# Last stages of an AdaLN and mixture-of-experts kernel: three sets of token blocks instead of two halves, strips of 256 tokens in the last two

## The chip, the cores and the metric

One core of a Trainium2 chip runs the whole program. The metric is the device time of one execution in microseconds (us). Data are float32 throughout.

## The reference

The input is 32 sequences of 128 tokens with 128 features, 4096 tokens. Two layers follow each other, and each adds its result to the input. The change touches the second layer (L1) only, so the first is given in one line.

```python
x = x + ffn0(cond0(x))                      # layer 0: gated experts with 512 hidden features
# layer 1, conditional part, for every token
shared = sum(silu(x @ w1[e].T) * (x @ w3[e].T) @ w2[e].T for e in range(2)) / 2    # hidden 256
routed = sum(gelu(x @ r1[e].T) @ r2[e].T * gate[:, e] for e in range(8))           # hidden 128
y = (shared + routed) / 4
# layer 1, low-rank part (rank 32, hidden 512)
p = y @ U1
h = gelu_tanh(p @ V1 + b1)
q = h @ U2
x = x + q @ V2 + b2
```

The gates of the routed experts come from a router that picks two of eight for each token; the kernel computes every expert for every token and multiplies by the gate, which is zero for the others.

## The kernel before

Tokens are kept transposed: features on the 128 partitions, tokens along the free dimension, in eight blocks of 512 tokens (`TB`), four blocks to a half (`SB = 4`, two halves). Layer 0 ends at about 825 us. What follows is a list of units that `pipelined` (L200) works through: it calls the first step (`up`) of unit i + 1, then the second step (`down`) of unit i, then whatever `after` (L926) hangs on unit i. The order of the list (L916 to L924) is thus the order of the program; within it a scheduler may still move an instruction of an engine ahead of another that it does not depend on.

There are three kinds of units. A shared unit (`sh_up`, L846) takes one 128-wide piece of the hidden features of the shared experts, for the four blocks of a half: for each block two products `g1` and `u1`, silu of the first on ScalarE, and the product of both on VectorE into the tile `hs`. A routed unit (`r_up`, L869) takes one routed expert: for each block the gate row is broadcast to all partitions by GpSimd (`spread`, L634, tile `rg`), one product `ur`, exact gelu on ScalarE (`ar`), and the multiply by the gate on VectorE (`hr`). Both kinds end in `into` (L841). The down projection and the rank-32 projection U1 have been folded beforehand into one matrix of 128 x 32 for each unit (`fold`), so `into` adds 32 rows for each block into one PSUM tile `p_ps`: block j of the half stands on partitions 32j to 32j + 31, all units of the half accumulate there. These matmuls use 32 columns of the array each, four side by side. The wide products are also cut into four matmuls of 32 columns (`by_columns`, L231).

A low-rank unit (`low_up`, L889, and `low_down`, L899) takes 128 of the 512 hidden features of the low-rank part: for each of the four strips one matmul `ul` from its 32 partitions of `pT` (the copy of `p_ps` in SBUF, `low_in`, L884), so 32 rows of the array and all columns, then gelu (tanh form, another table of ScalarE than silu and than exact gelu) with a bias into `hl`, and back by `into` to 32 rows in the PSUM tile `q_ps`. `low_out` (L904) copies `q_ps` to `qT`, does the last product `o_ps`, adds bias and residual on VectorE (`fin`, L912), and sends each block to HBM, in turn from the SP and the ScalarE queue.

The order of the units is: shared units of both halves; the eight routed units of half 0; two of half 1; three low-rank units of half 0; the other six routed units of half 1; the last low-rank unit of half 0; the four low-rank units of half 1; and `low_out(1)`.

Buffers in rotation: products in PSUM (`mm`) six, PSUM sums (`p_ps`, `q_ps`) two, `h` tiles (`hs`, `hr`, `hl`) three, outputs of ScalarE (`s1`, `ar`) four, broadcast gates four, `fin` four.

Of the kernel before, what the change touches and what calls it, by code (L numbers as in the profile page):

```python
# [44 lines left out]
SB = 4  # L45
NS = NB // SB
NT = B * S // P
H = 512
NC = H // P
E0, EF, E1 = 4, 8, 8  # L50
# [43 lines left out]
AT32, NCOLS32 = columns(COLS32)  # L94
# [5 lines left out]
def adaln_ffn(  # L100
# [3 lines left out]
    nc = tc.nc  # L104
    V = nc.vector
# [4 lines left out]
    work = ctx.enter_context(tc.tile_pool(name="work", bufs=2))  # L110
# [14 lines left out]
    par32 = const([P, NCOLS32], "par32")  # L125
# [12 lines left out]
    ident = const([P, P], "ident")  # L138
# [92 lines left out]
    def by_columns(ps, w, x, n):  # L231


        for at in range(0, P, n):
            own = slice(at, at + n)
            nc.tensor.matmul(ps[own, :], lhsT=w[:, own], rhs=x, start=True, stop=True)  # L236

# [3 lines left out]
    fold = const([P, 4 + E1, 32], "fold")  # L241
# [312 lines left out]
    def gates_to_dram(kind, sb):  # L554

        gates, name = held.pop((kind, sb)), f"{kind}g{sb}"
        ps = mm_tile(f"{name}_ps")
        nc.tensor.transpose(ps[:, :P], gates.rearrange("p e b -> p (e b)"), ident)
        t = work.tile([P, P], F32, tag="gsb", name=f"{name}_sb", bufs=1)
        V.tensor_copy(t, ps[:, :P])  # L560
        d = dram.tile([P, P], F32, tag=name, name=name)
        nc.sync.dma_start(out=d, in_=t)
        in_dram[kind, sb] = d.rearrange("(g k b) t -> k g (b t)", g=2, k=4)
# [44 lines left out]
    held, in_dram, fgates = {}, {}, {}  # L608
# [20 lines left out]
    units = [("s", b) for b in range(FIRST)] + [("p", q) for q in range(NUNIT)]  # L629
# [4 lines left out]
    def spread(row, name):  # L634

        bc = work.tile([P, TB], F32, tag="bc", name=name, bufs=4)
        nc.gpsimd.partition_broadcast(bc, row)  # L637
        return bc

    def glu(ps_gate, ps_up, h, name):  # L640
        s = work.tile([P, TB], F32, tag="sg", name=name, bufs=4)
        nc.scalar.activation(s, ps_gate, AF.Silu)  # L642
        V.tensor_tensor(h, s, ps_up, ALU.mult)  # L643
# [178 lines left out]
    sws_t = [wpool.tile([P, 2, 2, P], F32, tag=f"sw{i + 1}", name=f"sws{i}") for i in range(2)]  # L822
    rw1_t = wpool.tile([P, E1, P], F32, tag="w3", name="rw1_t")
# [3 lines left out]
    x1T = xT  # L827
# [8 lines left out]

    low_p = [y_tile(f"p_ps{sb}") for sb in range(NS)]

    def into(y, w, h, first, last):  # L841

        for j in range(SB):
            nc.tensor.matmul(y[32 * j : 32 * (j + 1), :], lhsT=w, rhs=h[:, j, :], start=first, stop=last)  # L844

    def sh_up(sb, k):  # L846
        e, c = divmod(k, 2)
        h = work.tile([P, SB, TB], F32, tag="h", name=f"hs_{sb}_{k}", bufs=3)
        for j in range(SB):
            x = x1T[SB * sb + j]  # L850
            g, u = mm_tile(f"g1_{sb}_{k}_{j}"), mm_tile(f"u1_{sb}_{k}_{j}")
            by_columns(g, sws_t[0][:, e, c, :], x, 32)
            by_columns(u, sws_t[1][:, e, c, :], x, 32)
            glu(g, u, h[:, j, :], f"s1_{sb}_{k}_{j}")
        return h

    def sh_down(sb, k, h):
        into(low_p[sb], fold[:, k, :], h, k == 0, False)


    grows = [
        wpool.tile([P, 2, SB * TB], F32, tag=tag, name=f"grows{sb}") for sb, tag in enumerate(("wg", "wu"))
    ]

    def gate_rows(sb):
        for k in range(4):
            nc.sync.dma_start(out=grows[sb][32 * k : 32 * k + 1, :, :], in_=in_dram["r", sb][k : k + 1, :, :])

    def r_up(sb, e):  # L869
        h = work.tile([P, SB, TB], F32, tag="h", name=f"hr_{sb}_{e}", bufs=3)  # L870
        g, k = divmod(e, 4)
        for j in range(SB):
            gate = spread(grows[sb][32 * k : 32 * k + 1, g, j * TB : (j + 1) * TB], f"rg_{sb}_{e}_{j}")
            ps = mm_tile(f"ur_{sb}_{e}_{j}")
            by_columns(ps, rw1_t[:, e, :], x1T[SB * sb + j], 32)
            a = work.tile([P, TB], F32, tag="sg", name=f"ar_{sb}_{e}_{j}", bufs=4)
            nc.scalar.activation(a, ps, AF.Gelu)  # L877
            V.tensor_tensor(h[:, j, :], a, gate, ALU.mult)  # L878
        return h

    def r_down(sb, e, h):
        into(low_p[sb], fold[:, 2 * 2 + e, :], h, False, e == E1 - 1)

    def low_in(sb):  # L884
        t = work.tile([P, TB], F32, tag="pT", name=f"pT{sb}", bufs=1)
        V.tensor_copy(t, low_p[sb])
        held["p", sb] = t

    def low_up(sb, c):  # L889
        h = work.tile([P, SB, TB], F32, tag="h", name=f"hl_{sb}_{c}", bufs=3)  # L890
        at = AT32["v1"].start + c * P
        for j in range(SB):
            ps = mm_tile(f"ul_{sb}_{c}_{j}")
            own = slice(32 * j, 32 * (j + 1))
            nc.tensor.matmul(ps, lhsT=par32[own, at : at + P], rhs=held["p", sb][own, :], start=True, stop=True)  # L895
            nc.scalar.activation(h[:, j, :], ps, AF.Gelu_apprx_tanh, bias=col("b1", c))
        return h

    def low_down(sb, c, h):  # L899
        if c == 0:  # L900
            held["q", sb] = y_tile(f"q_ps{sb}")
        into(held["q", sb], col("u2", c * 32, 32), h, c == 0, c == NC - 1)

    def low_out(sb):  # L904
        q = work.tile([P, TB], F32, tag="lgT", name=f"qT{sb}", bufs=1)
        V.tensor_copy(q, held["q", sb])
        for j in range(SB):
            ps = mm_tile(f"o_ps{sb}_{j}")
            own = slice(32 * j, 32 * (j + 1))
            nc.tensor.matmul(ps, lhsT=par32[own, AT32["v2"]], rhs=q[own, :], start=True, stop=True)  # L910
            t = work.tile([P, TB], F32, tag="fin", name=f"fin{sb}_{j}", bufs=4)
            V.scalar_tensor_tensor(t, ps, col("b2"), x1T[SB * sb + j], ALU.add, ALU.add)  # L912
            queue = nc.sync if j % 2 == 0 else nc.scalar
            queue.dma_start(out=out[SB * sb + j], in_=t)

    STAGES = {"s": (sh_up, sh_down), "r": (r_up, r_down), "l": (low_up, low_down)}  # L916
    units = [("s", sb, k) for sb in range(NS) for k in range(4)]
    units += [("r", 0, e) for e in range(E1)]
    units += [("r", 1, 0), ("r", 1, 1)]
    units += [("l", 0, c) for c in range(NC - 1)]  # L920
    units += [("r", 1, e) for e in range(2, E1)]

    units += [("l", 0, NC - 1)]
    units += [("l", 1, c) for c in range(NC)]  # L924

    def after(kind, sb, i):  # L926
        if (kind, sb, i) == ("s", 0, 0):
            gate_rows(0)

            l1_scores(1)  # L930
        if (kind, sb, i) == ("s", 0, 2):
            route(1)
        if (kind, sb, i) == ("s", 1, 0):
            gates_to_dram("r", 1)
            gate_rows(1)
        if kind == "r" and i == E1 - 1:
            low_in(sb)
        if (kind, sb, i) == ("l", 0, NC - 1):
            low_out(0)

    def unit_up(kind, *at):
        return STAGES[kind][0](*at)
# [1 line left out]
    def unit_down(kind, *at):  # L944
        STAGES[kind][1](*at)

    pipelined(units, unit_up, unit_down, after)
    low_out(1)


# [77 lines left out]
```

## Time and profile before

| what | value |
|---|---|
| median of 3 runs | 978.38 us (978.09 to 978.49) |
| profiled execution, its own time | 979.06 us |
| its span, first to last instruction | 977.3 us |
| mean granted clock of TensorE | 0.998 |
| routed experts: `ur`, records of TensorE | 512, of 592 ns |
| `p_ps` and `q_ps` records | 192 and 64, of 592 ns |
| `ul` records | 64, of 588 ns |
| gelu of the low-rank part, 128x512 | 32 times, 689 ns |
| exact gelu of the routed part, 128x512 | 64 times, 597 ns |
| multiply by the gate on VectorE | 64 times, 674 to 1152 ns |
| broadcast on GpSimd | 64 times, 797 to 1340 ns |
| final add on VectorE (`fin`) | 8 times, 743 ns |
| table loads of ScalarE after 820 us | 6, of 1283 ns |

A matmul of float32 appears as two records in the trace. Records of the same engine overlap: those of four neighbouring column or row groups of 32 run at the same time, so the duration of a record says how long it is in the array, and the distance between the starts of groups says what it costs. A weight load (PEld) of the next matmul runs beside the matmul before it where the trace shows the two overlapping.

### The profile page before, as it was taken

What the parts mean: (1) busy time and instruction counts of PE and PEld (TensorE: products, weight loads), DVE (VectorE), ACT (ScalarE), POOL (GpSimd) and SP (SyncE); (2) the same over time, 40 slices, a digit from 0 to 9 for tenths busy, and PEclk for the clock granted to TensorE, in tenths of its full rate; (3) what the DMA queues carried; (4) which work ended last, traced back from release to release, by engine and by line L of the source; (5) the groups of instructions that cost most, each with busy time, mean ns of one, the idle gap of its engine ahead of it and who ended that gap; (6) DMA issues with size and microseconds to landing.
All of it is one profiled execution on the core that took longest, in us unless ns stands there. A gap on an engine that the chain in (4) does not pass through costs nothing.

```text
span 977.3 us, 15574 instructions
## 1 busy us (share of the span) xinstructions
PE 962.9 (99%) x5998; PEld 450.8 (46%) x5998; DVE 630.5 (65%) x1130; ACT 345.0 (35%) x615; POOL 142.2 (15%) x151
## 2 busy tenths in 40 slices
PE   7999999999999999999999999999999999999997
PEld 3588974444444444444444444444444443323342
DVE  3444565666866776686676786567667656648593
ACT  5455544223322322232232332222223224335764
POOL 1000001100101011110101011010100001009680
PEclk9999999999999999999999999999999999999999
DMA  9745650000000000000000000000000000000002
GB/s 319 234 132 153 211 182 26 2 1 4 2 1 1 1 1 1 1 2 1 1 2 1 1 2 3 1 1 1 1 1 2 1 3 2 1 7 1 2 1 87
DMA packets 19043, 34.05 MB, mean 35 GB/s; under 512 B 1729, under 2 KB 9921, under 8 KB 18945
## 3 DMA queue, kind: packets, MB, share of 16 engines
q1 hardware_dynamic: 18096, 31.43, 10.3%
q10 hardware_dynamic: 864, 1.52, 0.4%
q8 instruction: 52, 0.85, 0.4%
q14 instruction: 31, 0.25, 0.1%
HBM read 30.59 MB, written 2.36 MB: 34 GB/s over the span
## 4 chain that ended last, share of the span: by engine, by line
PE 84%; DVE 2%; DVEq 0%; issue 0%
PE u L236 25%; PE g L236 25%; PE ya L729 10%; PE yb L729 8%; PE ur L236 6%; PE p_ps L844 2%; PE ul L895 1%; PE us L260 1%; PE ys L271 1%; PE q_ps L844 1%; PE y L513 0%; PE u L497 0%; DVE hf L704 0%; PE fold_ps L247 0%; DVE t L705 0%; DVE t L706 0%
## 5 line engine op out<-in xcount | busy, mean ns | idle before, releaser
L642 ACT ACTIVATE sf<-g 128x512 f32<-128x512 f32 x256 | 152.7, 597 | 438.1 <-PE g L236 432.0
L643 DVE TENSOR_TENSOR hf<-sf,u 128x512 f32<-128x512 f32 x256 | 174.9, 686 | 185.7 <-PE u L236 184.7
L236 PE MATMUL g<-c0all,wg_t 128*64 128x512 f32 x1024 | 270.3, 593 | 0.0
L236 PE MATMUL u<-cg,wu_t 128*64 128x512 f32 x1024 | 270.1, 592 | 0.0
L637 POOL PARTITION_BROADCAST fg<-fgT x64 | 71.9, 1135 | 662.4 <-DVE cg L685 499.1
L236 PEld LDWEIGHTS u<-cg,wu_t 128*64 128x64 f32 x1024 | 75.7, 137 | 145.2 <-issue 124.4
L236 PEld LDWEIGHTS g<-c0all,wg_t 128*64 128x64 f32 x1024 | 75.7, 137 | 120.2 <-issue 108.2
L729 PE MATMUL ya<-t,wd_t 128*64 128x256 f32 x512 | 121.6, 379 | 0.1
L637 POOL PARTITION_BROADCAST rg<-grows x64 | 67.8, 1187 | 145.4 <-DVE hr L878 76.8
L878 DVE TENSOR_TENSOR hr<-ar,rg 128x512 f32<-128x512 f32 x64 | 60.7, 996 | 15.8 <-ACT ar L877 15.8
L729 PEld LDWEIGHTS ya<-t,wd_t 128*64 128x64 f32 x512 | 69.9, 137 | 0.7 <-DVE t L706 0.6
L500 ACT ACTIVATE h<-u,w 128x256 f32<-128x256 f32 (+3 forms) x136 | 50.3, 429 | 54.3 <-PE u L497 54.3
L729 PE MATMUL yb<-hf,a_sum 128*64 128x256 f32 x512 | 69.1, 379 | 0.0
L729 PE MATMUL ya<-t,a_sum 128*64 128x256 f32 x256 | 65.9, 379 | 0.0
L729 PE MATMUL ya<-hf,wd_t 128*64 128x256 f32 x256 | 65.8, 379 | 0.0
L704 DVE TENSOR_TENSOR hf<-hf 128x512 f32<-128x512 f32 x64 | 62.7, 979 | 2.1
L236 PE MATMUL ur<-xall,rw_t 128*32 128x512 f32 x512 | 58.4, 592 | 0.0
L729 PEld LDWEIGHTS ya<-hf,wd_t 128*64 128x64 f32 x256 | 34.9, 137 | 42.8 <-issue 31.9
L513 PE MATMUL y<-h,w 128*128 128x256 f32 (+3 forms) x272 | 53.1, 338 | 1.0 <-DVE t L516 1.0
L497 PE MATMUL u<-x,w 128*128 128x256 f32 (+3 forms) x272 | 53.0, 338 | 1.1 <-DVEq L478 1.1
L497 PEld LDWEIGHTS u<-x,w 128*128 128x128 f32 x272 | 45.3, 190 | 5.7 <-ACT h L500 1.3
L877 ACT ACTIVATE ar<-ur 128x512 f32<-128x512 f32 x64 | 37.9, 598 | 27.6 <-PE ur L236 27.3
(215 smaller groups left out, 961.4 us busy)
## 6 DMA issues: line engine op xcount, KB each, us to landing
w<-in_experts SPq DMA_DIRECT2D x36, 514.5 KB
xall<-in_x SPq DMA_DIRECT2D x8, 256.0 KB
wg_t<-in_w_gate SPq DMA_DIRECT2D x8, 256.0 KB
wu_t<-in_w_up SPq DMA_DIRECT2D x8, 256.0 KB
wd_t<-in_w_down SPq DMA_DIRECT2D x8, 256.0 KB
out<-fin SPq DMA_DIRECT2D x4, 256.0 KB
out<-fin ACTq DMA_DIRECT2D x4, 256.0 KB
downs<-in_r_w SPq DMA_DIRECT2D x2, 256.0 KB
```

What stands on the lines that cost most here:

```text
L236: nc.tensor.matmul(ps[own, :], lhsT=w[:, own], rhs=x, start=True, stop=True)
L497: nc.tensor.matmul(ps[c][:, :m, :n], lhsT=w1, rhs=x[:, :m, :n], start=True, stop=True)
L500: nc.scalar.activation(h[:, c, :m, :n], ps[c][:, :m, :n], AF.Gelu_apprx_tanh, bias=bias)
L513: nc.tensor.matmul(y[:, :m, :n], lhsT=w2, rhs=h[:, c, :m, :n], start=(c == 0), stop=(c == NC - 1))
L637: nc.gpsimd.partition_broadcast(bc, row)
L642: nc.scalar.activation(s, ps_gate, AF.Silu)
L643: V.tensor_tensor(h, s, ps_up, ALU.mult)
L704: V.tensor_tensor(b12, b12, b11, ALU.subtract)
L729: nc.tensor.matmul(y[half, n], lhsT=w[:, c, :], rhs=h[:, c, :], start=False, stop=(e == EF - 1 and last))
L844: nc.tensor.matmul(y[32 * j : 32 * (j + 1), :], lhsT=w, rhs=h[:, j, :], start=first, stop=last)
L877: nc.scalar.activation(a, ps, AF.Gelu)
L878: V.tensor_tensor(h[:, j, :], a, gate, ALU.mult)
```

## The change

The eight blocks are now three sets (`group` in the code): set 0, blocks 0 to 3 as before; set 1, blocks 4 and 5; set 2, blocks 6 and 7. In the last two sets the four strips of 32 partitions in `p_ps`, `q_ps`, `pT` and `qT` hold half a block each, 256 tokens, so `p_ps` and `q_ps` matmuls, `ul` and the low-rank gelu are 256 wide there. A shared unit of these sets takes two blocks; a routed unit takes two experts with two blocks each, so it still has four products. The low-rank units of a set stand among the shared units of the next one: two shared, two low-rank, two shared, then two low-rank (after set 0) or one (after set 1, whose last one comes behind all routed units). The output of set 0 is made after the first routed unit of set 1, all on the SP queue; the output of set 1 among the low-rank units of set 2. The gates of the second half go to HBM and back after the second routed unit of set 0. For the last set, the residual of two of the four half blocks is put into PSUM ahead of time by a matmul with the identity (`out_begin`); ScalarE finishes these two with the bias, VectorE the other two, and each half block is sent by itself (`out_end`). All matmuls of 32 columns or 32 rows in these stages are kept in the order in which the program states them.

```diff
@@ by_columns
-            nc.tensor.matmul(ps[own, :], lhsT=w[:, own], rhs=x, start=True, stop=True)
+            mm = nc.tensor.matmul(ps[own, :], lhsT=w[:, own], rhs=x, start=True, stop=True)
+            if n < 64:
+                tc.keep_in_program_order(mm)
...
+    GROUPS = ((0, 4, TB), (4, 2, TB // 2), (6, 2, TB // 2))
+    low_p, low_q_ps = {}, {}
+    def in_order(mm):
+        tc.keep_in_program_order(mm)
-    def into(y, w, h, first, last):
-        for j in range(SB):
-            nc.tensor.matmul(y[32 * j : 32 * (j + 1), :], lhsT=w, rhs=h[:, j, :], start=first, stop=last)
+    def into(y, w, strips, first, last):
+        for j, h in enumerate(strips):
+            in_order(nc.tensor.matmul(y[32 * j : 32 * (j + 1)], lhsT=w, rhs=h, start=first, stop=last))
+    def strips_of(h, group):
+        n = GROUPS[group][2]
+        return [h[:, b, at : at + n] for b in range(h.shape[1]) for at in range(0, TB, n)]
...
+    def experts_of(group, i):
+        return (i,) if group == 0 else (2 * i, 2 * i + 1)
+    def r_up(group, i):
+        h = work.tile([P, SB, TB], F32, tag="h", name=f"hr_{group}_{i}", bufs=3)
+        pieces = [(e, b) for e in experts_of(group, i) for b in blocks(group)]
...
+    def r_down(group, i, h):
+        n = GROUPS[group][1]
+        for at, e in enumerate(experts_of(group, i)):
+            own = h[:, at * n : (at + 1) * n, :]
+            into(low_p[group], fold[:, 2 * 2 + e, :], strips_of(own, group), False, e == E1 - 1)
...
+    def by_rows(ps, w, t, j, first=True):
+        own = slice(32 * j, 32 * (j + 1))
+        in_order(nc.tensor.matmul(ps, lhsT=par32[own, w], rhs=t[own, :], start=first, stop=True))
+    def low_up(group, c):
+        h = work.tile([P, SB, TB], F32, tag="h", name=f"hl_{group}_{c}", bufs=3)
+        n = GROUPS[group][2]
+        v1 = AT32["v1"].start + c * P
+        for j in range(SB):
+            ps = mm_tile(f"ul_{group}_{c}_{j}")[:, :n]
+            by_rows(ps, slice(v1, v1 + P), held["p", group], j)
+            tc.keep_in_program_order(
+                nc.scalar.activation(h[:, j, :n], ps, AF.Gelu_apprx_tanh, bias=col("b1", c))
+            )
+        return h
...
+    def low_out(group, strips):
+        for j in strips:
+            b, at = strip(group, j)
+            ps = mm_tile(f"o_ps{group}_{j}")[:, : at.stop - at.start]
+            by_rows(ps, AT32["v2"], held["qT", group], j)
+            if at.start == 0:
+                t = work.tile([P, TB], F32, tag="fin", name=f"fin{b}", bufs=4)
+            V.scalar_tensor_tensor(t[:, at], ps, col("b2"), x1T[b][:, at], ALU.add, ALU.add)
+            if at.stop == TB:
+                nc.sync.dma_start(out=out[b], in_=t)
+    def out_begin():
+        for j in (1, 3):
+            b, at = strip(2, j)
+            held["o", j] = mm_tile(f"o_x{b}")[:, : TB // 2]
+            in_order(nc.tensor.matmul(held["o", j], lhsT=ident, rhs=x1T[b][:, at], start=True, stop=False))
+    def out_end():
         for j in range(SB):
+            b, at = strip(2, j)
+            ps = held["o", j] if j % 2 else mm_tile(f"o_ps{b}")[:, : TB // 2]
+            by_rows(ps, AT32["v2"], held["qT", 2], j, first=j % 2 == 0)
+            t = work.tile([P, TB], F32, tag="fin", name=f"fin_{j}", bufs=4)
+            if j % 2 == 0:
+                V.scalar_tensor_tensor(t[:, at], ps, col("b2"), x1T[b][:, at], ALU.add, ALU.add)
+                nc.sync.dma_start(out=out[b][:, at], in_=t[:, at])
+            else:
+                nc.scalar.activation(t[:, at], ps, AF.Identity, bias=col("b2"))
+                nc.scalar.dma_start(out=out[b][:, at], in_=t[:, at])
...
-    units = [("s", sb, k) for sb in range(NS) for k in range(4)]
-    units += [("r", 0, e) for e in range(E1)]
-    units += [("r", 1, 0), ("r", 1, 1)]
-    units += [("l", 0, c) for c in range(NC - 1)]
-    units += [("r", 1, e) for e in range(2, E1)]
-    units += [("l", 0, NC - 1)]
-    units += [("l", 1, c) for c in range(NC)]
+    units = [("s", 0, k) for k in range(4)] + [("r", 0, e) for e in range(E1)]
+    for group in (1, 2):
+        before_r = [("s", group, k) for k in range(4)]
+        low = [("l", group - 1, c) for c in range(NC)]
+        units += before_r[:2] + low[:2] + before_r[2:] + (low[2:] if group == 1 else low[2:3])
+        units += [("r", group, i) for i in range(E1 // 2)]
+    units += low[3:] + [("l", 2, c) for c in range(NC)]
...
-        if (kind, sb, i) == ("s", 1, 0):
+        if (kind, sb, i) == ("r", 0, 1):
             gates_to_dram("r", 1)
             gate_rows(1)
-        if kind == "r" and i == E1 - 1:
+        if kind == "r" and experts_of(sb, i)[-1] == E1 - 1:
             low_in(sb)
-        if (kind, sb, i) == ("l", 0, NC - 1):
-            low_out(0)
+        if kind == "l" and i == NC - 1:
+            low_q(sb)
+        if (kind, sb, i) == ("r", 1, 0):
+            low_out(0, range(SB))
+        if (kind, sb, i) == ("l", 2, 0):
+            low_out(1, (0, 1))
+        if (kind, sb, i) == ("l", 2, 1):
+            low_out(1, (2, 3))
+        if (kind, sb, i) == ("l", 2, 2):
+            out_begin()
...
-    low_out(1)
+    out_end()
```

More of the change, by code (lines that the diff above doesn't have):

```diff
@@ L834, in adaln_ffn, with blocks, sh_up, sh_down @@
         rest.pop(0)()
-    low_p = [y_tile(f"p_ps{sb}") for sb in range(NS)]
-    def into(y, w, h, first, last):
-        for j in range(SB):
-            nc.tensor.matmul(y[32 * j : 32 * (j + 1), :], lhsT=w, rhs=h[:, j, :], start=first, stop=last)
-    def sh_up(sb, k):
-        e, c = divmod(k, 2)
[L848 to L854, printed above, removed]
-        return h
-    def sh_down(sb, k, h):
-        into(low_p[sb], fold[:, k, :], h, k == 0, False)
+    GROUPS = ((0, 4, TB), (4, 2, TB // 2), (6, 2, TB // 2))
[8 more added lines that the diff above has]
+        return [h[:, b, at : at + n] for b in range(h.shape[1]) for at in range(0, TB, n)]
+    def blocks(group):
+        first, n, _ = GROUPS[group]
+        return range(first, first + n)
+    def sh_up(group, k):
+        e, c = divmod(k, 2)
+        h = work.tile([P, SB, TB], F32, tag="h", name=f"hs_{group}_{k}", bufs=3)
+        for at, b in enumerate(blocks(group)):
+            g, u = mm_tile(f"g1_{b}_{k}"), mm_tile(f"u1_{b}_{k}")
+            by_columns(g, sws_t[0][:, e, c, :], x1T[b], 32)
+            by_columns(u, sws_t[1][:, e, c, :], x1T[b], 32)
+            glu(g, u, h[:, at, :], f"s1_{b}_{k}")
+        return h
+    def sh_down(group, k, h):
+        _, n, size = GROUPS[group]
+        if k == 0:
+            low_p[group] = y_tile(f"p_ps{group}")[:, :size]
+        into(low_p[group], fold[:, k, :], strips_of(h[:, :n, :], group), k == 0, False)
     grows = [
@@ L867, in gate_rows @@
             nc.sync.dma_start(out=grows[sb][32 * k : 32 * k + 1, :, :], in_=in_dram["r", sb][k : k + 1, :, :])
-    def r_up(sb, e):
-        h = work.tile([P, SB, TB], F32, tag="h", name=f"hr_{sb}_{e}", bufs=3)
-        g, k = divmod(e, 4)
-        for j in range(SB):
[L873 to L878, printed above, removed]
-        return h
@@ L881, in r_down @@
[L881 to L891, printed above, removed]
-        for j in range(SB):
[L893 to L914, printed above, removed]
@@ new lines, in r_up @@
+    def r_up(group, i):
+        h = work.tile([P, SB, TB], F32, tag="h", name=f"hr_{group}_{i}", bufs=3)
+        pieces = [(e, b) for e in experts_of(group, i) for b in blocks(group)]
+        for at, (e, b) in enumerate(pieces):
+            g, k = divmod(e, 4)
+            sb, j = divmod(b, SB)
+            gate = spread(grows[sb][32 * k : 32 * k + 1, g, j * TB : (j + 1) * TB], f"rg_{b}_{e}")
+            ps = mm_tile(f"ur_{b}_{e}")
+            by_columns(ps, rw1_t[:, e, :], x1T[b], 32)
+            a = work.tile([P, TB], F32, tag="sg", name=f"ar_{b}_{e}", bufs=4)
+            nc.scalar.activation(a, ps, AF.Gelu)
+            V.tensor_tensor(h[:, at, :], a, gate, ALU.mult)
+        return h
@@ new lines, in r_down, with low_in @@
+    def r_down(group, i, h):
[3 more added lines that the diff above has]
+            into(low_p[group], fold[:, 2 * 2 + e, :], strips_of(own, group), False, e == E1 - 1)
+    def low_in(group):
+        t = work.tile([P, TB], F32, tag="pT", name=f"pT{group}", bufs=1)[:, : GROUPS[group][2]]
+        V.tensor_copy(t, low_p[group])
+        held["p", group] = t
+    def by_rows(ps, w, t, j, first=True):
+        own = slice(32 * j, 32 * (j + 1))
+        in_order(nc.tensor.matmul(ps, lhsT=par32[own, w], rhs=t[own, :], start=first, stop=True))
@@ new lines, in low_up, with low_down @@
+    def low_up(group, c):
+        h = work.tile([P, SB, TB], F32, tag="h", name=f"hl_{group}_{c}", bufs=3)
+        n = GROUPS[group][2]
+        v1 = AT32["v1"].start + c * P
+        for j in range(SB):
+            ps = mm_tile(f"ul_{group}_{c}_{j}")[:, :n]
[3 more added lines that the diff above has]
+            )
+        return h
+    def low_down(group, c, h):
+        n = GROUPS[group][2]
+        if "q" not in low_q_ps:
+            low_q_ps["q"] = y_tile("q_ps")
+        strips = [h[:, j, :n] for j in range(SB)]
+        into(low_q_ps["q"][:, :n], col("u2", c * 32, 32), strips, c == 0, c == NC - 1)
@@ new lines, in low_q, with strip @@
+    def low_q(group):
+        n = GROUPS[group][2]
+        q = work.tile([P, TB], F32, tag="lgT", name=f"qT{group}", bufs=1)[:, :n]
+        V.tensor_copy(q, low_q_ps["q"][:, :n])
+        held["qT", group] = q
+    def strip(group, j):
+        first, n, size = GROUPS[group]
+        b, half = divmod(j, SB // n)
+        return first + b, slice(half * size, (half + 1) * size)
+    def low_out(group, strips):
[8 more added lines that the diff above has]
+                nc.sync.dma_start(out=out[b], in_=t)
```

## The prediction

> **What bounds the kernel now.** I read the page first, then a table by stage of the last 100 us, then the chain of waits, and last the timelines of ScalarE, VectorE and GpSimd in the same place.
>
> ```profile
> span 977.3 us, 15574 instructions
> ...
> PE 962.9 (99%) x5998; PEld 450.8 (46%) x5998; DVE 630.5 (65%) x1130; ACT 345.0 (35%) x615; POOL 142.2 (15%) x151
> ...
> PE 84%; DVE 2%; DVEq 0%; issue 0%
> ```
>
> TensorE sets the time over the whole program; the first 825 us are not touched, so only the last 152 us count. The table by stage (busy PE, PEld, DVE, ACT, POOL, then granted clock, DMA share, GB/s):
>
> ```profile
> 875.00:918.00 43.00, 43.00 (x408) 12.84 (x400) 36.09 (x41) 24.39 (x42) 39.51 (x38) 1.00 0.01 2
> 918.00:925.10 7.10, 7.10 (x55) 2.40 (x56) 1.39 (x2) 7.07 (x12) 2.71 (x3) 1.00 0.00 0
> 925.10:950.00 24.90, 24.90 (x236) 12.56 (x232) 21.68 (x22) 15.92 (x27) 20.90 (x20) 1.00 0.01 2
> 950.00:977.30 27.30, 20.33 (x112) 5.68 (x104) 9.71 (x14) 13.81 (x22) 0.57 (x1) 0.92 0.21 77
> ```
>
> The last 27.3 us are a tail: TensorE counts as busy but does 112 records, where 24.9 us of routed experts hold 236. ScalarE fills the second row. The chain (start, us) shows what the pieces cost:
>
> ```profile
> 917.16 0.86 PE p_ps L844 x8
> 918.02 1.07 PE ul L895 x8
> 919.09 1.40 PE p_ps L844 x8
> ...
> 946.55 3.43 PE ur L236 x32
> 949.99 0.86 PE p_ps L844 x8
> ...
> 966.12 3.45 PE q_ps L844 x15
> ...
> 970.34 1.18 PE o_ps L910 x8
> ```
>
> A group of four strips of 512 tokens (8 records) takes 0.858 (3.43/4); I call it Q. The low-rank matmuls use 32 rows, the others 32 columns: going in costs about 0.2 (1.07 against 0.86), coming out 0.13 to 0.2. The `q_ps` of 3.45 is one Q stretched by waiting for ScalarE.
>
> ```profile
> 917.84 1.28 ACT L896 ACT_TABLE_LOAD   x1
> 919.14 7.17 ACT L896 ACTIVATE hl<-ul,par 128x512 f32<-128x512 f32 x12
> 926.33 1.28 ACT L877 ACT_TABLE_LOAD   x1
> ```
>
> Twelve activations in 7.17, 0.57 apart in the steady part: four need 2.3, more than the 1.7 of their two Q. And in the routed stage:
>
> ```profile
> 928.32 9.84 DVE L878 TENSOR_TENSOR hr<-ar,rg 128x512 f32<-128x512 f32 x10 [8.94 <-ACT ar L877]
> 929.10 9.72 POOL L637 PARTITION_BROADCAST rg<-grows  x9 [8.40 <-DVE hr L878]
> ```
>
> After two free starts (0.60 apart) a multiply by the gate and a broadcast move in step, 1.067 us a pair: 4.27 for the four of a unit, against 4.29 on TensorE (five Q). VectorE has no room there to make up a delay.
>
> **The change, part by part.** I count Q up to the end of the last `ur`, which is 949.99 before, then the tail.
>
> *Work moved.* From 825.03 to 949.99 the old order does 48 Q of shared `g`/`u`, 8 of their `p_ps`, 1 of `l_ps`, 64 of `ur`, 14 of their `p_ps`, 3 of `ul`, 3 of `q_ps`: 141 Q, 121.0 us; the other 3.9 are 1.4 at `l_b`, 0.3 at `rg_ps`, 1.9 in the low-rank block (7.08 for six Q), and rounding. The new order does before its last `ur` the same 48, 8, 1, 64, 14, and 5.5 `ul`, 5.5 `q_ps`, 1 `o_ps` (a 256-wide group is half a Q): 147 Q, or **+5.15**.
>
> That a 256-wide group runs at full rate is not shown for 32 columns. The nearest row is L729 (128x256, 64 columns): pairs of records 0.216 apart, weight loads of 137 ns hidden. I take 0.216 for four records of 32 columns, whose loads are shorter (110). Ends: nothing, or the load exposed, 0.11 on each of 46 such record groups (16 of shared units, 24 of routed, 6 of `q_ps`), 5.1 us. A gain is excluded, the array does the same columns.
>
> *Overheads in front of the last `ur`.* `l_b`, `rg_ps`: 1.9, 0.2 more than before, because the lone `p_ps` strip that ran while VectorE copied `l1T` is now pinned behind it. Set 0's low-rank units, first pair, time from the end of the last `u`: `p_ps` to 0.43, `ul` with its switch to 1.5; the tanh table is there at 1.1 (silu ends 0.2 before `u` does in this trace, load 1.28, small gap); four activations from 1.7 end at 4.1; only then can the last strip of `q_ps` start, end 4.95. Ideal is four Q, 3.43, so 1.5 lost. Second pair: here the listing of waits puts a PE wait on the table load itself, so it starts after `ul` (1.8), activations from 3.1, `q_ps` ends 6.3: 2.9 lost. `o_ps` of set 0 between routed units: two switches, 0.4. Set 1's first pair, half as wide (0.36 an activation, below): 1.0; its third unit: 0.4. Sum 8.1 against 3.9, **+4.2**. The other table loads (14 in these stages instead of 6) lie beside at least 3.4 us of `g`/`u` or `ur`, with six PSUM buffers in rotation; without that cover they would be 1.28 each.
>
> Here a rule speaks against the change. The Trainium skill (ScalarE: Activation LUTs, What ACT_TABLE_LOAD costs) counts about 1.38 us of drain on top of 1283 ns for each switch. The trace has the load at 926.33, right behind an activation that ends at 926.32, and the next activation at 927.62: 1.29 from end to start. By the row, the two loads in front of `q_ps` cost what stands above; by the rule those and the two that delay the last routed stage would add 4 x 1.4, 5.5 us. I take the row.
>
> *The four output adds of set 0* (`fin`, 0.66 apart) and the `qT` copy now sit on VectorE among set 1's multiplies, 3.3 us where it has no spare time. `p_ps` of a unit comes 4.29 after that unit's last `ur`; its multiply normally ends about 1.9 after it, and `o_ps` gives another 1.3. Behind the adds are queued eight multiplies; by my count they end 0.1 to 0.8 before their strips of `p_ps` can start. So nothing; from 0 to +0.7 if the adds compete with broadcasts (multiplies with a PSUM operand, L643, keep 686 ns beside broadcasts, so I take 0). Their DMAs go to SP, with nothing behind that is awaited. Set 1's gates (transpose `rg_ps`, a copy, five DMAs on SP) move from the second shared unit to the second routed one of set 0, where they are issued near 856 and first read near 905: hidden by ten units; without that cover each us of their way would be a us of set 1's routed stage.
>
> T1, the end of the last `ur`: 949.99 + 5.15 + 4.2 = 959.3.
>
> *The tail.* Old: 27.3 from T1. New: ahead of the last routed stage lie, on ScalarE, a tanh load that waits for `ul`, four activations and a gelu load, so the first gelu runs 3.7 after its `ur` starts (876.03 - 874.92 = 1.1 for set 0 before). Multiplies start 2.6 late and, at 4.27 against 4.29, stay late: the last ends T1+3.6 (before 952.18, T1+2.2). `p_ps` of its strips, then `pT` at 4.4, `ul` at 5.0, first activation 5.5. Sixteen activations of 128x256: four of 128x172 take 1.29, so 0.296 apart, and 512 wide 0.571; the line between gives 0.36 (ends 0.30 and 0.43, the pace of L500 at 256, which its matmuls set). They end at 12.0. The two identity matmuls (128 columns, 0.86) stand in front of the last `q_ps`, which starts at 12.6 instead of 12.1; `qT` 13.3, `o_ps` 13.9, then activation, DMA issue, activation, second issue at 15.8. The same laying-out of the old tail ends 0.4 too early; added. From last issue to end was 977.29 - 974.25 = 3.04 with 256 KB; with 128 KB I take 2.8 (2.4 to 3.04). Tail 19.0: **-8.3**.
>
> Sum: 5.15 + 4.2 - 8.3 = +1.05, span 978.3 to 978.4. The profiled execution took 979.06, 0.68 over the median of 978.38. 978.38 + 1.05 is 979.4; the same durations laid out instruction by instruction, without rounding, give 0.2 more, so **979.6**.
>
> **Rivals.** *Narrow groups are slower* (ends slower). Place: `p_ps` and `q_ps` at 256 columns, 46 record groups on the path. Price 0.11 if loads are exposed (984.7). The same page set (TensorE: Matmul & The Clock Gate, "Wait — 56ns, not 53.3ns?") has about 62 ns of issue per matmul in one mode, 0.248 a group instead of 0.216: +1.5, 981.1. Against it: the gate matmuls of 128x4 start 30 to 40 ns apart at 19.9 us. It decides from 0.016 a group. *The lag grows*: VectorE loses more in the last two routed stages (adds against broadcasts, load waits) and each us comes out at the end: 980.5 to 982. *The tail gives all*: set 0's second load is early (-1.4), the lag of the last multiply falls back to 2.2 (-1.4), activations run at 0.30 (-0.7): 976.1. For it: VectorE idled 16% from 875 to 918. *The strips don't shorten ScalarE's block* (a fixed cost rules, 0.43 each): 16 x 0.07 more, 980.7.
>
> **Chances.** Measurement can tell about 0.2%, 1.96 us. Near cancelling, 976.4 to 980.3: 0.46. Slower: 0.42 (narrow groups 0.15, lag or wide activations 0.22, table drain 0.05). Faster: 0.12. Range for eight in ten: 977.0 to 983.2; the likeliest case alone is 977.5 to 980.3.
>
> **What would show it.** Last `ur` ends near 959.3, `q_ps` behind each pair of `ul` waits for `hl`; 8 records of 128x256 `p_ps` take 0.43; 14 table loads; first gelu of the last set 3.7 after its `ur`; `pT` of the last set 4.4 after T1, tail 19. Wrong if narrow records start more than 0.06 apart on average, or if the last multiply ends within 2.2 of T1.

## The result, and the profile after

The changed kernel takes 982.57 us (median of five, 981.10 to 982.97), the kernel before 978.23. The estimate of the ratio is 1.0039, with an interval from 1.0027 to 1.0052 (the quotient of the two medians, 1.0044, lies inside). It is slower by more than the 0.2 % that can be told from no change. The likeliest case of the prediction (within 0.2 %, 979.6) did not come. The time lies in the range of 977.0 to 983.2, but partly by luck: the largest part of the excess is a halved clock of TensorE, for which neither the sum nor any of the rivals had a term.

Names used from here on: pair A and pair B are the first two and the last two low-rank units of set 0, pair C the first two of set 1. A row switch is the change of TensorE between matmuls of 32 columns and of 32 rows. "Full clock" means a granted clock of 1.00. Q is the prediction's 0.858 us.

The profiled execution took 982.97; its page begins so:

```profile
span 981.2 us, 15957 instructions
...
PE 965.7 (98%) x6170; PEld 456.6 (47%) x6170; DVE 628.6 (64%) x1134; ACT 358.4 (37%) x641; POOL 141.3 (14%) x151
```

The span grew by 3.9, TensorE's busy time by 2.8. The table by stage, whose last row stands against the 27.3 us of tail before:

```profile
885.95:906.25 20.30, 19.83 (x156) 7.84 (x152) 3.35 (x5) 15.37 (x23) 0.00 (x0) 0.93 0.00 1
...
961.10:981.20 20.10, 13.53 (x136) 6.24 (x127) 7.75 (x14) 10.73 (x25) 2.23 (x3) 0.94 0.15 53
```

The tail did shrink. The last row begins 0.37 before the end of the last `ur` (961.47); counted from that end, as for the 27.3, the tail is 19.7. The first row is the stretch of set 0's low-rank units: the column after POOL is the granted clock, and it is 0.93, where before no row outside the tail was under 1.00. The chain there, pair A and pair B, then the output of set 0:

```profile
885.95 0.43 PE p_ps L854 x8
886.38 1.07 PE ul L922 x8
...
888.02 1.89 PE ul L922 x8
889.90 1.08 PE q_ps L854 x8
...
898.71 0.43 PE p_ps L854 x8
...
902.31 2.07 PE ul L922 x4
904.38 1.87 PE q_ps L854 x8
906.25 3.84 PE ur L236 x32
...
915.24 1.07 PE o_ps L922 x8
916.31 3.77 PE ur L236 x32
```

Pair A loses 1.6, as forecast (1.5). Pair B takes 7.54 from its first `p_ps` to the end of `q_ps` and so loses 4.1 against its ideal four Q, where 2.9 was forecast. In it eight records of `q_ps` take 1.87 instead of the Q of 0.86, though they no longer wait, and the 32 records of `ur` behind them take 3.84 instead of 3.43. Single microseconds of the table by stage show why:

```profile
902.20:903.20 1.00, 0.89 (x3) 0.58 (x4) 0.00 (x0) 1.00 (x3) 0.00 (x0) 1.00 0.03 8
...
904.20:905.20 1.00, 1.00 (x9) 0.23 (x12) 0.00 (x0) 1.00 (x3) 0.00 (x0) 0.50 0.00 0
...
907.20:908.20 1.00, 1.00 (x14) 0.24 (x10) 0.00 (x0) 0.57 (x1) 0.00 (x0) 1.00 0.00 0
```

From 903.52 to 906.93, for 3.41 us, TensorE is granted half its clock. The trace of before has no such stretch until 973.13, when its last matmul is over.

### The profile page after: what moved, and what is told of

Its sections match the earlier page's. It is cut to its first block, busy times and chain, and to the rows that moved or that the text cites. A ratio compares the mean times of both kernels' runs of the same rounds, so it can differ in the third digit from the quotient of the medians.

```text
span 981.2 us, 15957 instructions
## 1 busy us (share of the span) xinstructions
PE 965.7 (98%) x6170; PEld 456.6 (47%) x6170; DVE 628.6 (64%) x1134; ACT 358.4 (37%) x641; POOL 141.3 (14%) x151
## 4 chain that ended last, share of the span: by engine, by line
PE 96%; DVE 2%; DMA 1%; ACT 0%; issue 0%; ACTq 0%; DVEq 0%; SPq 0%
PE u L236 25%; PE g L236 25%; PE ya L731 10%; PE yb L731 8%; PE ur L236 6%; PE u L499 5%; PE y L515 5%; PE us L262 3%; PE ys L273 3%; PE p_ps L854 2%; PE ul L922 1%; PE q_ps L854 1%; DMA w<-in_experts 1%; DMA sw_t<-in_sw 0%; PE o_ps L922 0%; DVE hr L905 0%
## 5 line engine op out<-in xcount | busy, mean ns | idle before, releaser
L731 PEld LDWEIGHTS yb<-hf,a_sum 128*64 128x64 f32 x512 | 38.6, 137 | 18.5
```

The source lines that it names most:

```text
L731: nc.tensor.matmul(y[half, n], lhsT=w[:, c, :], rhs=h[:, c, :], start=False, stop=(e == EF - 1 and last))
```

## The experiments

Two readings stood at first. *Clock*: pair B's excess is the halved clock, and ScalarE's wait is as forecast. *ScalarE alone*: the tanh activations hold up more than was laid out. To compare traces, T1 (end of the last `ur` record) is counted here from the end of layer 0's last matmul, since that falls between 809.9 and 811.4 from trace to trace (811.16 before and 810.85 in the changed kernel; the "about 825" given for it earlier is where the first `p_ps` of the shared units starts). The tail runs from T1 to the end. The ratios are estimates over all executions and need not equal the quotient of the medians beside them.

| kernel | median (lowest to highest) | kernel before, median on the same chip | ratio, interval | T1 from layer 0 | tail |
|---|---|---|---|---|---|
| before | 978.23 | | | 138.83 | 27.30 |
| changed | 982.57 (981.10 to 982.97) | 978.23 | 1.0039, 1.0027 to 1.0052 | 150.62 | 19.73 |
| changed, again | 983.33 (981.53 to 984.09) | 978.32 | 1.0048, 1.0034 to 1.0061 | 150.56 | 19.70 |
| filling in pair B | 981.73 (980.61 to 981.87) | 978.73 | 1.0030, 1.0020 to 1.0041 | 149.31 | 19.70 |
| filling in pair A | 982.61 (982.23 to 982.79) | 978.32 | 1.0042, 1.0028 to 1.0056 | 150.45 | 19.76 |
| pair B apart | 981.09 (979.86 to 981.69) | 978.73 | 1.0024, 1.0013 to 1.0034 | 149.29 | 19.56 |
| own buffers at the end | 980.83 (980.31 to 982.37) | 978.73 | 1.0026, 1.0015 to 1.0037 | 149.32 | 19.88 |
| all single | 978.06 (977.05 to 979.00) | 978.73 | 0.9993, 0.9985 to 1.0001 | 147.26 | 18.60 |
| early tables | 978.60 (977.51 to 979.30) | 978.15 | 1.0002, 0.9993 to 1.0010 | 147.91 | 18.41 |
| later output | 983.00 (one execution) | 978.15 | | 151.42 | 19.91 |
| combined, pairs in set 0 | 978.72 (977.93 to 979.83) | 978.15 | 1.0002, 0.9994 to 1.0010 | 148.17 | 18.57 |
| combined, all single | 979.58 (978.30 to 980.30) | 978.15 | 1.0013, 1.0007 to 1.0020 | 148.50 | 18.54 |
| pairs, set 1 single | 978.71 (978.15 to 979.63) | 978.32 | 1.0004, 0.9995 to 1.0012 | 147.48 | 18.68 |
| three in a row | 979.23 (978.16 to 979.94) | 978.32 | 1.0006, 0.9998 to 1.0014 | 147.84 | 18.69 |

### Filling in pair B

```diff
+    def fill():
+        for _ in range(2):
+            for j in range(SB):
+                own = slice(32 * j, 32 * (j + 1))
+                in_order(nc.tensor.matmul(low_p[1][own], lhsT=fold[:, 0, :], rhs=x1T[4][:, : TB // 2],
+                                          start=False, stop=False))
@@ low_up
+            if (group, c, j) == (0, 3, 2):
+                fill()
```

> The changed kernel with 16 more records of TensorE in the second pair of low-rank units of set 0: two groups of four 128x256 matmuls of 32 columns, 0.86 us at full rate, put just ahead of the third `ul` of unit 3, where TensorE waits for a PSUM buffer (901.84 to 902.31 in the changed kernel). They add products of block 4 to `p_ps` of set 1, so blocks 4 and 5 come out with another value; nothing else differs. Theory (clock): in the changed kernel TensorE's granted clock is 0.50 for one stretch of 3.41 us from 903.5 on, because TensorE had little to do in the 3.4 us before it. `q_ps` of unit 2 (1.71 for eight records instead of 0.86) and the first `ur` (0.46 longer) run at half speed, and the last `ul` ends 0.37 late. With the filling the stretch does not come; ScalarE's wait is the same and hides the filling. The first `ur` starts near 904.9 instead of 906.0, and the time falls by 1.2 to 1.7 us against the changed kernel, to about 981.0, although it does more. Rival (ScalarE alone): what pair B lost beyond the forecast is longer waiting for the tanh activations; then the filling changes nothing or costs up to 0.9: 982.5 to 983.4.

No halved stretch in its trace; `q_ps` starts at 904.05, `ur` at 904.93, T1 is 1.31 earlier than in the changed kernel, although 16 records were added. Against the kernel before on its chip it is slower by 3.0, the changed kernel by 4.3. The size of the clock's share is as expected. That the filling is what kept the stretch away is not shown by this run: in the next one the stretch is absent without it.

### Own buffers at the end

```diff
-            t = work.tile([P, TB], F32, tag="fin", name=f"fin_{j}", bufs=4)
             if j % 2 == 0:
+                t = work.tile([P, TB], F32, tag="fin", name=f"fin_{j}", bufs=4)
...
+                t = work.tile([P, TB // 2], F32, tag=f"end{j}", name=f"fin_{j}", bufs=1)
```

> The changed kernel with own buffers for the two half blocks that ScalarE finishes (two tiles of 128x256), so that its last activation waits for TensorE alone; before, it waits for four things (two DMAs, VectorE and TensorE), because its buffer came round from an earlier block. Theory: the 0.46 us between the end of ScalarE's first DMA issue (977.07) and its second activation (977.53) are waits that the rotation of the `fin` buffers put there; all of what it waits for is done by 977.04. Without them the activation starts at 977.1, the last DMA issue at 977.6, and the span is 0.4 shorter: time 0.3 to 0.5 less than the changed kernel, if the stretch of halved clock is there as often. Rival (queue): the 0.46 is what a ScalarE queue needs after a DMA issue before the next activation; then nothing changes.

Nothing in this kernel touches pair B, and its profiled execution has no halved stretch. Its PE timeline (start, us, records, what it waited for), which is the changed kernel's pair B at full clock:

```profile
902.86 1.70 PE L922 MATMUL ul<-pT,par 32*128 32x512 f32 x4 [0.47 <-ACT hl L933]
904.49 1.15 PE L854 MATMUL q_ps<-hl,par 128*32 128x512 f32 x8
905.38 3.70 PE L236 MATMUL ur<-xall,rw_t 128*32 128x512 f32 x32
```

and the same records of the changed kernel:

```profile
902.31 2.07 PE L922 MATMUL ul<-pT,par 32*128 32x512 f32 x4 [0.47 <-ACT hl L933]
904.31 1.94 PE L854 MATMUL q_ps<-hl,par 128*32 128x512 f32 x8
```

The wait for ScalarE ahead of the third `ul` is 0.47 in both. What differs is the length of the records behind it, and T1 by 1.30. So "ScalarE alone" falls for this excess: the halved clock accounts for all of it. It comes in some executions only. Totals alone would not show this: the end of layer 0 varies by 1.5 us between traces, and this profiled execution took 982.37 without the stretch, 1.5 above its kernel's median.

As to the end: the timelines of ScalarE, changed first, then this kernel, show the second activation's idle time.

```profile
977.53 0.47 ACT L986 ACTIVATE fin<-o_x,par 128x256 f32<-128x256 f32 x1 [0.86 <-DVE fin L983]
978.03 0.35 ACTq L987 DMA_DIRECT2D out<-fin  x1
```

```profile
975.95 0.37 ACTq L988 DMA_DIRECT2D out<-fin  x1
976.37 0.48 ACT L987 ACTIVATE fin<-o_x,par 128x256 f32<-128x256 f32 x1 [0.45 <-ACT fin L987]
```

It fell from 0.86 to 0.45, of which 0.37 is the DMA issue: 0.41 gained, as expected, so the rotation of four `fin` buffers had put the wait there. (All that the activation waited for had been done by 977.04; why the wait lasts 0.41 all the same stays open.) In time this cannot be told apart; the last DMA landed 3.72 after its issue here and 3.17 in the changed kernel, which takes the gain back in these two traces.

### The changed kernel again, and filling in pair A

The second kernel has the condition `(group, c, j) == (0, 1, 2)` in place of `(0, 3, 2)`.

> The changed kernel once more, unchanged, on the chip of the three runs beside it, as their measure. Theory (clock): its executions fall into two groups, 1.3 to 1.9 us apart, by whether the 3.41 us stretch of halved clock falls into pair B: near 981.0 with a mean granted clock of 0.998 to 1.0, near 982.6 with 0.996 or 0.997. Rival: one group, and the mean clock doesn't go with the time.

> The same 16 filling records as in the run with the filling, but in pair A, where TensorE waits too and where no trace shows the clock halved. Blocks 4 and 5 come out with another value, as there. A placebo for that run: same records, same values, other place. Theory (TensorE too idle in the 3.4 us ahead of the stretch): pair B stays as it is, the stretch comes in part of the executions, 982.4 to 983 with mean clock 0.996 or 0.997 there, as often as in the changed kernel itself. Rival (the filling run was merely lucky, or it is the work and not its place): no execution at 0.997, all near 981.5.

The changed kernel's ten executions, on two chips, fall into two groups: eight with a mean clock of 0.997 take 982.14 to 984.09 (mean 983.03), two with 0.999 take 981.10 and 981.53 (mean 981.32). That is 1.7 apart, beside 1.3 in the traces; the theory's point holds.

The placebo did not behave as the theory said: none of its five executions shows 0.997. It was also no clean placebo. In pair A the filling was not hidden (`q_ps` there starts 1.23 later, T1 1.13 later than at full clock), so pair B moved by 1.2 us, and 982.61 is the time at full clock plus that. So with a filling in B (eight executions) and in A (five) the stretch stayed away, and in the kernel with own buffers it came in two of seven. That it is TensorE's sparse work in pair B that calls it is argued, not shown.

What is shown: in all three traces that have the stretch (the changed kernel twice, and the later output) it lasts 3.41 and begins 894.29 us, 262 times 3.413, after the clock's first release. That release falls between 7.5 and 11.1 us after the start in the 14 traces. The clock's fall after the last matmul also comes a whole number of 3.413 us after the release in all 14. The stretch thus sits on a grid that begins at the release, and pair B lies differently to it from one execution to the next. The Trainium skill (TensorE: Matmul & The Clock Gate, Part 1: The HAM clock gate) describes such a free-running window of 3413 ns and half the clock after an idle window; length and factor agree. But TensorE was not idle in the grid's window right ahead of the stretch. That window in the changed kernel, then the same one (number 261) in the trace with own buffers, where no halving follows:

```profile
900.10:903.51 3.41, 2.94 (x20) 1.04 (x16) 0.00 (x0) 3.22 (x5) 0.00 (x0) 1.00 0.01 2
```

```profile
901.93:905.34 3.41, 2.94 (x16) 1.04 (x16) 0.00 (x0) 3.40 (x7) 0.00 (x0) 1.00 0.01 2
```

TensorE counts as busy for 2.94 us in both (and in the other two traces that have the stretch), and for only 2.30 in the window from 132.10 of the changed kernel, which no halving follows either. So the busy time of that window alone does not decide, and how little work is enough is not answered by that page nor by these runs.

### Pair B apart, and all single

```diff
@@ pair B apart (group 1)
+            units += before_r[:2] + low[:2] + [before_r[2], low[2], before_r[3], low[3]]
@@ all single
+        units += before_r[:2] + [low[0], before_r[2], low[1], before_r[3], low[2], routed[0]]
+        units += (low[3:] if group == 1 else []) + routed[1:]
```

(`routed` is the list of a set's routed units. In "all single" set 0's output also moves, behind the second routed unit of set 1.)

> The changed kernel with the second pair of low-rank units of set 0 taken apart: shared unit 2, low-rank 2, shared unit 3, low-rank 3, instead of both shared units and then both low-rank units. Two more table loads on ScalarE (16 instead of 14). Theory: TensorE never waits for two times four tanh activations in a row. Each of the two single units costs about 0.4 (two switches between 32 rows and 32 columns), the sum 0.8 instead of the 4.1 + 0.46 of the pair, and no stretch of granted clock 0.50. T1 (end of the last `ur`) about 957.4 instead of 961.15, time 978.8. Rival (ScalarE's pace rules wherever the units stand): the extra loads, 2 x 1.28, and the late silu hold up `g`/`u` through the six PSUM buffers; then only the clock's share comes back, 1.3 to 1.7, and the time is 981 or more.

> The changed kernel with every low-rank unit of sets 0 and 1 standing by itself: shared 0, shared 1, low 0, shared 2, low 1, shared 3, low 2, routed 0, and for set 0 low 3 after that, its output after the second routed unit. Theory: pair A of set 0 lost 1.6, pair B 4.6, pair C of set 1 1.2; as singles about 0.4 each, so 4 x 0.4 + 2 x 0.4 = 2.4 instead of 7.4, no stretch at clock 0.50: time about 977.5, below both kernels. Rival (routed stage has no room): low 3 of set 0 between the first routed units delays their gelu by two loads and four activations (4.8 on ScalarE against 2.1 on TensorE), VectorE and GpSimd can't make it up at 1.067 us a pair, and `p_ps` of the following units wait about 1 to 2.7 us: 978.5 to 980.2, not better than the kernel in which only pair B is taken apart.

Taking pair B apart gained nothing over the changed kernel at full clock: T1 is 149.29 beside 149.32, and the time is 981.09 where the theory had 978.8 and the rival 981 or more. The rival's number was right. ScalarE's timeline of that kernel has hardly a gap left:

```profile
895.97 1.28 ACT L933 ACT_TABLE_LOAD   x1 [1.81 <-PE ul L922]
897.26 2.42 ACT L933 ACTIVATE hl<-ul,par 128x512 f32<-128x512 f32 x4
899.70 1.28 ACT L644 ACT_TABLE_LOAD   x1
901.00 1.09 ACT L644 ACTIVATE s<-g 128x512 f32<-128x512 f32 x2
902.10 1.28 ACT L933 ACT_TABLE_LOAD   x1
```

Load, four tanh, load, two silu take 6.13 (902.10 - 895.97), while TensorE's work of one shared and one single low-rank unit is six and a half Q, 5.6, and the two row switches. A single unit pays two loads for four activations, so ScalarE stays full. Still, up to the `ur` ahead of set 0's output this kernel is 0.8 earlier than the one with own buffers (101.15 beside 101.97 after layer 0). It loses the same 0.8 right behind `o_ps`, where half a unit's `ur` waits for an add (with own buffers first, then with pair B apart):

```profile
917.41 1.92 PE L236 MATMUL ur<-xall,rw_t 128*32 128x512 f32 x16 [0.25 <-DVE fin L964]
```

```profile
916.38 1.92 PE L236 MATMUL ur<-xall,rw_t 128*32 128x512 f32 x16 [1.04 <-DVE fin L964]
```

So a small gain was there, and set 0's output took it; the wait changed its place.

With all units single T1 came 2.06 earlier than at full clock with pairs, and the tail was 1.1 shorter. Some of this may come from the output's new place, which no run takes apart. From the first shared unit of set 2 to T1 it took 0.7 less than the pairs did: there the activations are half as wide (1.57 for four), and ScalarE has room for two loads. This version is level with the kernel before: 0.9993, interval up to 1.0001. Its time of 978.06 lies between the theory (977.5) and the rival (978.5 to 980.2).

### Early tables

```diff
+    def table(fn):
+        t = work.tile([P, 1], F32, tag="tb", name="tb", bufs=1)
+        tc.keep_in_program_order(nc.scalar.activation(t, col("b1", 0), fn))
@@ r_up
+        if i == 0:
+            table(AF.Gelu)
@@ low_up
+        if c in (0, 2) and (group, c) != (2, 2):
+            table(AF.Gelu_apprx_tanh)
```

> The changed kernel with six extra activations of 128x1 on ScalarE whose only use is to bring the table earlier: tanh ahead of each pair (and of set 1's single third unit, and of set 2's first), exact gelu ahead of each set's first routed unit. Background: in the changed kernel the tanh load of pair B begins at 900.28, when `ul` is done, though ScalarE idles from 896.8 on; in pair A it begins right behind the last silu. In the experiment with single units nothing was gained over the clock's share, because there ScalarE was full (a load, four tanh, a load, two silu: 6.1 for every 5.9 of TensorE); so the loads are the scarce thing. Theory (place of the load): pair B loses 1.3 less, the stretch of halved clock (1.3 where it comes) does not come, set 1's third unit lets the first gelu of the last set start at about 947.6 instead of 948.95, so the last multiply lags 1.3 less and the tail is 18.7 instead of 20.05, pair C gains 0.2: 2.8 below the changed kernel at full clock (981.1), that is 978.3. Rival (lag set by VectorE and GpSimd): the multiplies stay as late as before since they move at 1.067 a pair whatever the gelu does; only pair B's 1.3 and 0.2 come back: 979.6. Second rival (the activations' pace of 0.57 and the six PSUM buffers set pair B): no more than 0.3: 980.8.

The changed kernel's ScalarE idles ahead of two tanh loads until `ul` is done; the third line is the exact gelu of the last set behind them:

```profile
900.28 1.28 ACT L933 ACT_TABLE_LOAD   x1 [1.79 <-PE ul L922]
...
944.77 1.28 ACT L933 ACT_TABLE_LOAD   x1 [1.36 <-PE ul L922]
...
948.95 3.05 ACT L904 ACTIVATE ar<-ur 128x512 f32<-128x512 f32 x6
```

With an activation of 128x1 ahead, which waits for nothing of TensorE's, the same places are

```profile
898.17 1.28 ACT L896 ACT_TABLE_LOAD   x1
...
940.68 1.28 ACT L896 ACT_TABLE_LOAD   x1
...
945.05 2.04 ACT L910 ACTIVATE ar<-ur 128x512 f32<-128x512 f32 x4
```

T1 is 1.41 earlier than at full clock in the changed kernel, the tail 1.3 shorter; 2.7 in all where 2.8 was expected, and no execution of 13 has a clock under 0.999. The theory (place of the load) stands, both rivals fall. It does not beat the kernel before (1.0002).

### Later output, and the combinations

The output of set 0 moved behind the first shared unit of set 2: `low_out(0, range(SB))` at `("s", 2, 0)` in place of `("r", 1, 0)`.

> The changed kernel with the output of set 0 (`o_ps`, four adds on VectorE, four DMAs) moved from behind the first routed unit of set 1 to behind the first shared unit of set 2. Theory: the prediction put these adds at nothing on TensorE's path; the profile of the changed kernel shows `ur` behind `o_ps` at 3.77 instead of 3.43 (3.91 where the clock was not halved before), so VectorE had no room for them and a PSUM buffer or a multiply came late. Moved, `ur` of the routed units is 3.43 throughout set 1 and the last `ur` ends 0.3 to 0.5 earlier, counted from the end of layer 0; the two switches of `o_ps` (0.3) stay. Rival: the 0.3 to 0.5 is the restart of `ur` after the row switch; then it moves along to the shared units and nothing is gained.

Theory and rival both missed the time. In set 1 `ur` is 3.43 throughout, so the loss there was indeed the adds, as the theory said; but T1 came 0.8 later (151.42 beside 150.62, both with the stretch). The timeline shows the new wait:

```profile
932.11 2.73 DVE L964 SCALAR_TENSOR_TENSOR fin<-o_ps,par,xall 128x512 f32<-128x512 f32 x4 [0.69 <-PE o_ps L922]
...
932.91 0.29 PEld L922 LDWEIGHTS ul<-pT,par 32*128 32x128 f32 x2 [0.81 <-DVE fin L964]
932.91 1.35 PE L922 MATMUL ul<-pT,par 32*128 32x256 f32 x4 [0.41 <-DVE fin L964]
```

Four `o_ps` hold four of six PSUM buffers until VectorE has added, 0.66 apart; `ul` of the next low-rank unit needs the third buffer at once.

Two combinations that had the later output in them ran beside it:

> All that the runs pointed to, in pairs for set 0: early tables (as in the run with the six small activations), output of set 0 among the shared units of set 2, set 1's low-rank units single, own buffers for ScalarE's two half blocks. Sum from the changed kernel at full clock (981.1): 2.8 for the tables, 0.4 for the output, 0.7 for set 1's singles (what the run with single units showed from the start of set 2 to T1), 0.4 for the buffers: 976.8. If the multiplies' lag is set by VectorE and GpSimd alone, 978.1. At or above 978.7 (the kernel before on this chip) the reading of the earlier runs is wrong.

> The same, but set 0's low-rank units single too (the fourth after the first routed unit of set 1), so the difference to the former is single against pairs in set 0 once the tables come early. Theory: ScalarE is full with singles (6.1 for every 5.9 us of TensorE), an early table brings nothing there, and pairs with early tables are 0 to 1.5 faster: about 977.5 here. Rival: singles remain ahead of pairs by the 1.3 that the runs without early tables showed: 975.5.

Both missed by 1.9 and more, and the first is not below the kernel before, so readings in its sum were wrong. That of the output is one, a gain of 0.4 that was a loss; two more come out below. T1 is 148.17 and 148.50. With all units single the table's early place brought nothing (as the theory said), and the combination is 1.24 later at T1 than all single alone, whose output stood behind the second routed unit. Pairs were ahead of singles by 0.9 in the medians, inside the theory's 0 to 1.5 (0.3 in the two traces).

```diff
@@ three in a row (group 1)
+            units += before_r + routed[:1] + low[:3] + routed[1:2] + low[3:] + routed[2:]
```

> The kernel with early tables, set 1's low-rank units single, own buffers for ScalarE's two half blocks; set 0's output stays behind the first routed unit of set 1. The combined run with the later output lost at `ul` of set 2, which waited for PSUM buffers that four `fin` of 0.66 on VectorE held (0.40, 0.81, 0.37). Theory: leaving the output where it was takes 1.1 off that run (2.1 lost behind `o_ps` there, 1.0 here), end 0.5 ahead of the kernel before: ratio 0.9994, about 0.5 us. Rival: singles of set 1 bring nothing once tables come early; then level with the kernel before.

> As the former, but set 0's low-rank units as in the kernel before: three in a row behind the first routed unit of set 1, the fourth behind the second; output behind the third. The last two sets with strips of 256 and the divided end stay. Theory: in a row of three, ScalarE pays one pair of table loads for twelve activations, TensorE loses 1.9 for three units (before) plus 0.4 for the fourth, instead of 1.6 + 1.4 for the two pairs: 0.7 ahead of the former, 1.2 ahead of the kernel before. Rival: the routed stage of set 1 has no room, the four adds and the late gelu shift VectorE and `p_ps` waits up to 2: 0.8 slower than the kernel before.

With the output back, T1 is 147.48 and the total 166.16 from layer 0's end, beside 166.13 in the kernel before: level, not 0.5 ahead. Beside early tables alone, set 1's singles and the own buffers together gave T1 0.43, and the tail took 0.27 of it back; the sum of the first combination had 0.7 for the singles and 0.4 for the buffers. These two and the output account for the larger part of its miss. The row of three lost 0.36 more at T1: twelve tanh activations in a row pay one pair of loads, but TensorE waits through them (the chain is on ScalarE from 896.7 to 907), and the adds came late. No version was measurably ahead of the kernel before.

## Where the prediction was right and where it was wrong

That the gain in the tail would be used up in front of T1, with a kernel somewhat slower, was right, and so were most terms. From the end of layer 0 the profiled execution grew by 4.2 us where the sum had 1.05, for the following reasons.

*TensorE's clock.* The sum took every duration at full clock. Pair B's step "`q_ps` ends 6.3: 2.9 lost" is right at full clock (6.4 and 2.9 in the trace with own buffers), but in eight of ten executions the halved clock comes on top, 1.3 by the traces and 1.7 by the totals. This missing term is the largest: the two executions without it lie near 981.3.

*The output of set 0, "0.4" and "so nothing".* At full clock (own buffers, and both fillings) `p_ps`, `o_ps` and `ur` take 5.96 there, against 5.15 without loss: 0.8. The count of VectorE's multiplies against `p_ps` had left out that `ur` needs the PSUM buffers which the four adds hold; the wait of 0.25 for `fin` above is that. 0.4 too little. (In the changed kernel's own trace the place takes 5.70: a part of what the clock cost is made up there, and 1.3 is what remains at T1.)

*The tail, 19.0.* Measured 19.73. Up to `o_ps` the laying-out holds (13.95 after T1, forecast 13.9). The second ScalarE activation waited 0.41 on account of its rotated buffer, which was not laid out, and the last DMA took 3.17 from its issue, not 2.8.

*Smaller terms.* Pair A 1.6 for 1.5, pair C 1.2 for 1.0, 0.2 of rounding that the prediction named, and 0.2 that I cannot place.

The sum: T1 moved by 11.79 (150.62 - 138.83) where 9.35 was forecast, so +2.4: clock 1.3, output 0.4, the smaller terms 0.7. The tail fell by 7.57 where 8.3 was forecast: +0.7. With the 1.05 of the prediction that is 4.2; layer 0 ended 0.3 earlier in this trace, and the span grew by 3.9.

*What held.* Eight records of 128x256 `p_ps` take 0.43 (885.95 above), so narrow groups are not slower, and that rival falls. The 14 table loads take 1.28 each with no drain beside them (the one at 962.31 ends at 963.59, and its activation starts at 963.60), so the row was the right choice against the rule on ScalarE. The first gelu of the last set starts 3.85 after its `ur` (forecast 3.7), and the last multiply ends at 964.94, 3.47 after T1 (forecast 3.6, and 2.2 named as the sign of being wrong). In two kernels the 16 multiplies of the last set take the same time, whenever they begin:

```profile
949.63 15.31 DVE L905 TENSOR_TENSOR hr<-ar,rg 128x512 f32<-128x512 f32 x16 [5.21 <-ACT ar L904]
```

```profile
946.43 15.31 DVE L911 TENSOR_TENSOR hr<-ar,rg 128x512 f32<-128x512 f32 x16 [4.23 <-issue]
```

The first is the changed kernel, the second the one with set 1's units single. So the rival of a growing lag falls as well; the lag is set where the multiplies begin. One reading was too strict here: "no room" on VectorE took 4.27 for four multiplies, and these take 3.83.

*Where the hoped-for gain went.* The tail gave 7.6 back. The work that filled it before (six Q) went in front of T1 for 5.15, which is no loss in itself. The 6.6 more at T1 (11.79 less 5.15) are waits of TensorE for ScalarE's tables and activations, row switches, buffers held by adds, and the clock.

## What to carry to other kernels

Moving work out of an idle tail pays only what the place it goes to does not charge: here each group of tanh activations among silu and gelu needs two loads of 1.28 us, whether it has four or eight of them, and a stage that had room by its busy share (VectorE, ScalarE) had none in its order. Look at the wait that stands ahead of a table load: if the first activation of the new function waits for TensorE, a tiny one ahead of it brings the load forward (2.7 us in this kernel). And where TensorE is made to stop and go, look at the granted clock of single microseconds, in more than one execution, before the excess is put down to the engine it waited for.

## What was not expected of the hardware

The granted clock halved for 3.41 us in the middle of a program whose TensorE counts as 98 % busy, at 894.29 us after its first release in three traces of three. Whether it strikes decides 1.3 to 1.7 us, and differs between executions of one kernel on one chip. Two windows with the same busy time, 2.94 of 3.41 us, were followed by a halved clock in one trace and not in the other. What keeps it away stays open.
